# A message-passing layer: the first node tile alone and picked from SBUF, the split of h and the last bias through PSUM

## The chip, the core and the metric

The kernel runs on one core of a Trainium2 chip. A core has five engines with queues of their own, each executed in order: TensorE (PE, matmuls into PSUM), VectorE (DVE), ScalarE (ACT), GpSimd (POOL) and SyncE (SP), which issues most transfers. SBUF is the working memory, PSUM takes the matmuls' results, DRAM holds inputs, outputs and tables. The metric is the device time of one execution in microseconds (us), lower is better. Five runs of the kernel before gave 4235.94 to 4246.19, median 4244.6.

## The reference

12500 nodes with 128 features, 412500 edges sorted by their target node `dst`, 20 edge features, one weight an edge.

```python
h = maximum(layernorm(x), 0)
h = h @ W_in2f
Wij = (softplus(f_ij @ W_f1 + b_f1) - LOG2) @ W_f2 + b_f2
Wij = Wij * rcut_ij[:, None]
agg = segment_sum(h[dst] * Wij, src)          # called with idx_i = src, idx_j = dst
out = x + (softplus(agg @ W_o1 + b_o1) - LOG2) @ W_o2 + b_o2
```

`dst` is sorted, so the rows of h that a run of edges reads lie close together. `src` isn't, so the messages go to scattered places.

## The kernel before, in words

**Chunks.** The edges go in 806 chunks of 512, four to a group. Every chunk passes these stages, each a method of `Group`:

- `hidden` (L666): for two chunks at a time, `z = W_f1 @ f` on PE, K = 20, the two chunks in two groups of rows of the array; `hidden_log` (L675) three ScalarE activations of 1024 columns, `hidden_end` (L683) one VectorE product. The result is `r`.
- `bias` (L767) and `value` (L779): PSUM tile `v` = bias + r @ W_f2, four PE matmuls (8 instructions, since float32 goes in two passes). For the first chunks the bias is put in by PE (L772), later by ScalarE (L776).
- `rows` (L617): a window of 32 rows of h, each stored as three bfloat16 parts, is read from a table in DRAM into `near`, from a start that SP loads from memory; `window` (L760) compares the edges' node numbers (relative to the chunk's first, `rel`) with row numbers; `pick` (L787) is one matmul for each 128 edges, of the comparison with `near`; `picked` (L794) scales by `rcut` on ScalarE, four activations of 128 columns (L799).
- `blocks` (L690), `rank` (L698), `rank_end` (L715): where each message goes. `inb` marks the block of 128 target nodes, matmuls with triangular matrices (L711, and L744 for the chunk before) count the places taken, a reduction (L716) and three small operations give `slot`. `columns` (L629) makes the numbers for eight groups at once.
- `message` (L803): VectorE multiplies `v` and `hg` into `o` (L810), and GpSimd issues four indirect DMAs (L814), each putting 128 messages into `slots` in DRAM: 3224 in all.

**Collecting.** While chunks go on, `Collect` reads the filled segments of `slots` back and sums them by matmuls (L865, L886). The last segment is collected after the last chunk, followed by the output stage (`finish`, L427), which adds `x`. `x_ahead` (L1075) loads `x` early: from chunk 300 on, the first 14 sets get the last bias added by VectorE (L425, `x_bias`), the others by GpSimd after its last indirect DMA. Slots are cleared by transfers of 387 KB (L1185), spread over the steps: one each at steps 0, 1, 2, 4, 5, 7, 8, 9 and so on.

**h.** `make_h(q)` (L326) makes four node tiles of 128 rows in six stages, parted by `yield`: statistics on VectorE and 1/sqrt by Ln and Exp on ScalarE (L337 to L342); a refinement and the centring and scaling of x on VectorE (L346 to L353); transposes on PE and Relu on ScalarE (L358, L360); the product with W_in2f (L364) and the first bfloat16 part (L366); `left` = h minus that part, on VectorE (L369), and the second part (L370); the third part (L372: `left` minus the second, both in SBUF), and the stores to the tables. Table 0 holds the first 512 rows and serves chunks 0 to 8; table 1 (896 rows) needs the second set too and serves chunks from 9 on. `NEXT` (L914) is 8, the last chunk of table 0.

**Order.** The program's order is written out by hand: every engine executes its instructions in the order in which the code emits them. The prologue (L1154 to L1179) makes the first set and chunk 0's hidden part; then `step(k)` (L972) is called for k = -3, -2, ... Step k emits chunk k's `message`, k + 1's `picked` and `value`, k + 2's `pick` and `bias`, k + 3's `window`, and up to six chunks ahead of `rows`, `blocks` and `rank`. After step k one stage of the first two sets is emitted (from k = -1), from k = 6 on one stage of `side()` (L1141): later sets, further loads, `rest()`. PSUM's eight banks: z two, acc one, v three (bias, picks and values in turn), one for the counts, one for the constant `count_ps`. `o` has four buffers of two chunks, so VectorE can be up to eight chunks ahead of GpSimd.

Of the kernel before, what the change touches and what calls it, by code (L numbers as in the profile page):

```python
# [17 lines left out]
P = 128  # L18
TG = 16
CH = 512  # L20
# [13 lines left out]
FIRST = 64  # L34
NEAR = 2 * P
# [7 lines left out]
def gnn_kernel(  # L43
# [33 lines left out]
    NFLAG = 6 * len(SEGS) + 9  # L77
# [66 lines left out]
    nbo1 = sbuf("nbo1", [P, 1])  # L144
    before = sbuf("before", [P, P])
# [26 lines left out]
    rows_at = NPART * CH * 3 // 2 + CH  # L172

# [9 lines left out]
    def load_x(q):  # L183
        n = min(QT, NTILE - q * QT)
        full = min(n, N // P - q * QT)
        xb = ln.tile([P, QT, P], F32, name="xb")
        if full < n:
            nc.vector.memset(xb[:, full:n, :], 0.0)
            nc.sync.dma_start(xb[:N % P, full, :], x[q * QN + full * P:N, :])
        if full:  # L190
            nc.sync.dma_start(xb[:, :full, :], x[q * QN:q * QN + full * P, :]
                              .rearrange("(c p) f -> p c f", p=P))
        return xb

# [59 lines left out]
    def constants():  # L254

        early[0] = load_x(0)
        part_load(0)
        first_load(0)
        nc.sync.dma_start(win, w_in2f)

        for j in range(NCHUNK):
            nc.sync.dma_start(wf1[32 * j:32 * j + RBF, :], w_f1)

        nc.scalar.preload_act_table_set("natural_log_exp_and_others")
        nc.scalar.dma_start(bf1, b_f1[:, None])
        nc.scalar.dma_start(wf2, w_f2)
        nc.scalar.dma_start(bf2, b_f2[None, :].to_broadcast([P, P]))
        make_identity(nc, ident)
# [4 lines left out]
        nc.gpsimd.iota(prow_i, pattern=[[0, 1]], base=0, channel_multiplier=43)  # L273
        nc.gpsimd.iota(places, pattern=[[1, P]], base=0, channel_multiplier=0,
# [27 lines left out]
    def biases(psum):  # L302

        nc.vector.tensor_scalar(nbf1, bf1, -1.0, None, op0=ALU.mult)
        b12 = psum.tile([P, QT, P], F32, name="b12", tag="acc")[:, 0, :]
# [20 lines left out]
    def make_h(q, psum):  # L326

        n = min(QT, NTILE - q * QT)
        xb = early.pop(q, None)
# [6 lines left out]
        for i in range(n):  # L336
            nc.vector.bn_stats(st[:, i, :], xb[:, i, :])  # L337
            nc.vector.bn_aggr(mv[:, i, :], st[:, i, :])

        rs = ln.tile([P, QT], F32, name="rs")  # L340
        nc.scalar.activation(rs[:, :n], mv[:, :n, 1], AF.Ln, bias=eps)
        nc.scalar.activation(rs[:, :n], rs[:, :n], AF.Exp, scale=-0.5)  # L342
        yield

        ve = ln.tile([P, QT], F32, name="ve")
        nc.vector.tensor_scalar(ve[:, :n], mv[:, :n, 1], EPS, -0.5, op0=ALU.add, op1=ALU.mult)  # L346
        r2 = ln.tile([P, QT], F32, name="r2")
        nc.vector.tensor_mul(r2[:, :n], rs[:, :n], rs[:, :n])
        nc.vector.tensor_mul(r2[:, :n], r2[:, :n], ve[:, :n])
        nc.vector.scalar_tensor_tensor(rs[:, :n], r2[:, :n], 1.5, rs[:, :n],  # L350
                                       op0=ALU.add, op1=ALU.mult)
        for i in range(n):
            nc.vector.tensor_scalar(xb[:, i, :], xb[:, i, :], mv[:, i, 0:1], rs[:, i:i + 1],  # L353
                                    op0=ALU.subtract, op1=ALU.mult)
        yield
        xps = psum.tile([P, QT, P], F32, name="xps", tag="acc")
        for i in range(n):
            nc.tensor.transpose(xps[:, i, :], xb[:, i, :], ident)  # L358
        xT = ln.tile([P, QT, P], F32, name="xT")
        nc.scalar.activation(xT[:, :n, :], xps[:, :n, :], AF.Relu)  # L360
        yield
        hps = psum.tile([P, QT, P], F32, name="hps", tag="acc")
        for i in range(n):
            nc.tensor.matmul(hps[:, i, :], xT[:, i, :], win, start=True, stop=True)  # L364
        hb = ln.tile([P, QT, 3, P], BF16, name="hb")
        nc.scalar.activation(hb[:, :n, 0, :], hps[:, :n, :], AF.Copy)  # L366
        yield
        left = ln.tile([P, QT, P], F32, name="left")
        nc.vector.tensor_sub(left[:, :n, :], hps[:, :n, :], hb[:, :n, 0, :])  # L369
        nc.scalar.activation(hb[:, :n, 1, :], left[:, :n, :], AF.Copy)  # L370
        yield
        nc.vector.tensor_sub(hb[:, :n, 2, :], left[:, :n, :], hb[:, :n, 1, :])  # L372
        for (b, rows), table in zip(tables, h3_t):
            lo = max(0, b - q * QN) // P
            hi = min(n, (b + rows - q * QN) // P)
            if lo < hi:
# [4 lines left out]
                if b + rows == QN:  # L381
                    yield
# [5 lines left out]
            h3[q * QN:q * QN + n * P, :].rearrange("(c p) f -> p c f", p=P),  # L388
            hb[:, :n, :, :].rearrange("p c k f -> p c (k f)"))
# [32 lines left out]
    def x_bias(xo, pieces, engine=nc.vector):  # L422
        for p, cs, rows in pieces:
            xi = xo[:p, cs, :]
            engine.tensor_add(xi, xi, spread(bo2[:p, :], xi.shape[1]))  # L425

    def finish(t0, n, sT, quad, psum, z, xo=None, bank=("v", 3)):  # L427

        pieces = x_pieces(t0, n)
        if xo is None:  # L430
            xo = quad.tile([P, QT, P], F32, name="xo", bufs=6)
            x_load(xo, pieces)
            x_bias(xo, pieces)
# [103 lines left out]
    with tc.tile_pool(name="edge", bufs=2) as edge, tc.tile_pool(  # L537
# [11 lines left out]
        count_ps = state_ps.tile([P, P], F32, name="count_ps")  # L549
# [33 lines left out]
        class Group:  # L583


            def __init__(self, g):
# [3 lines left out]
                if g % NB == 0:  # L590
                    f = edge.tile([P, NB, CH], F32, name="f")
                    for j in range(NCHUNK):
                        nc.sync.dma_start(f[32 * j:32 * j + RBF, :, :],
                                          f_t[g:g + NB, j].rearrange("b k n -> k b n"))
                    kept["f"] = f
                self.f = kept["f"][:, g % NB, :]
                i = g - self.seg.g0
                if i % SB == 0:
# [3 lines left out]
                    nc.sync.dma_start(src_i[:, :w], src_t[:, cols])  # L602
                    rcut = edge.tile([P, SB * TG], F32, name="rcut")
                    nc.sync.dma_start(rcut[:, :w], rcut_t[:, cols])
# [3 lines left out]
                if g == 0:  # L608
                    rel_store(0)
                self.rel = edge.tile([WP, NCHUNK, CH], BF16, name="rel", bufs=4)  # L610
                nc.sync.dma_start(self.rel, rel_d[g * NCHUNK:(g + 1) * NCHUNK, :][None, :, :]
                                  .to_broadcast([WP, NCHUNK, CH]))
# [3 lines left out]

            def rows(self, c):  # L617

                k = self.g * NCHUNK + c
                t = table_of[k]  # L620
# [8 lines left out]
            def columns(self):  # L629
                if len(self.cols) == 3:  # L630
# [677 lines left out]
```

## Time and profile before

| what | value |
|---|---|
| profiled execution, whole | 4243.52 us |
| its span, first to last instruction | 4241.8 us |
| median of five runs | 4244.6 us |
| POOL busy | 3146.0 us, 74% of the span |
| PE busy | 3369.1 us, 79% |
| VectorE busy | 3093.4 us, 73% |
| ScalarE busy | 2774.7 us, 65% |
| HBM traffic | 192 GB/s over the span |

Busy times of PE overlap, since matmuls are pipelined. A group's row gives the line, engine and operation, out<-in by the program's names, the count, the busy time, the mean duration in ns, and the engine's idle time just before its instructions with what ended most of it. "issue" is idle time that ends without a wait that the profile shows. A timeline row merges equal neighbours: its duration is from the first's start to the last's end.

### The profile page before, as it was taken

Reading aid. Unit: us, or ns where it says so; the run is one execution under the profiler, and the core shown is the slowest. Engines: PE = TensorE matmul, PEld = TensorE weight load, DVE = VectorE, ACT = ScalarE, POOL = GpSimd, SP = SyncE. Lnnn points to the kernel's source line nnn. Section 1 sums busy time; section 2 is a strip of 40 time slices with the busy share of each in tenths; the row PEclk is TensorE's granted clock in tenths of the full one; section 3 lists DMA queues with packets and bytes.
Section 4 is the critical chain, followed back from the end, with each engine's and each line's share of the span. In section 5 each row is a group of like instructions: output and inputs, shape, how many; then the busy total and the mean of one; then the engine's idle time right before and its main releaser. Section 6 shows DMA issues by size and latency. Waiting matters only on the chain. (4 is left out here: it accounts for less than half of the span.)

```text
span 4241.8 us, 72525 instructions
## 1 busy us (share of the span) xinstructions
PE 3369.1 (79%) x21598; PEld 2617.0 (62%) x21598; DVE 3093.4 (73%) x6698; ACT 2774.7 (65%) x5464; POOL 3146.0 (74%) x3292
## 2 busy tenths in 40 slices
PE   6666676766776676678888888888888988988888
PEld 4444454444444444467777777777777777776777
DVE  7766665666555555567778777887888888888877
ACT  6776676677666666666666666666666666766644
POOL 5777777777777777777777777777777777777772
PEclk9777766776666666689899999998998998999999
DMA  6665555545444344467778766778776876787766
GB/s 185 193 185 182 171 165 181 162 149 176 131 127 119 106 147 149 145 185 230 218 216 258 235 206 211 218 215 264 222 213 205 266 243 189 234 245 202 207 203 178
DMA packets 515212, 820.54 MB, mean 193 GB/s; under 512 B 177188, under 2 KB 312728, under 8 KB 514812
## 3 DMA queue, kind: packets, MB, share of 16 engines
q1 hardware_dynamic: 411212, 602.55, 49.1%
q0 software_dynamic: 103168, 213.15, 15.0%
q8 instruction: 175, 2.87, 0.3%
q14 instruction: 225, 1.84, 0.1%
q10 hardware_dynamic: 432, 0.13, 0.0%
HBM read 419.75 MB, written 395.69 MB: 192 GB/s over the span
## 5 line engine op out<-in xcount | busy, mean ns | idle before, releaser
L814 POOL DMA_INDIRECT slots<-o,slot x3224 | 3108.5, 964 | 1011.6 <-issue 756.3
L886 PEld LDWEIGHTS acc<-to,m 128*128 128x128 f32 x8152 | 1077.3, 211 | 244.8 <-issue 148.6
L799 ACT ACTIVATE hg<-picked,rcut 128x128 f32<-128x128 f32 x3224 | 909.9, 364 | 391.0 <-PE picked L791 238.1
L783 PEld LDWEIGHTS v<-wf,r 128*128 128x128 f32 x6448 | 1010.0, 236 | 245.8 <-issue 154.0
L886 PE MATMUL acc<-to,m 128*128 128x128 f32 x8152 | 1138.7, 299 | 25.1 <-DVE to L865 21.6
L783 PE MATMUL v<-wf,r 128*128 128x128 f32 x6448 | 1086.3, 323 | 10.6 <-ACT v L776 10.6
L671 PE MATMUL z<-f,wf 20*128 20x512 f32 x1612 | 595.4, 822 | 409.3 <-DVE r L687 408.0
L776 ACT ACTIVATE v<-bf 128x512 f32<-128x512 f32 x804 | 483.8, 602 | 596.9 <-DVE o L810 577.8
L865 DVE TENSOR_TENSOR to<-count_ps,m 128x640 f32<-128x640 f32 (+3 forms) x793 | 632.2, 823 | 48.9 <-PE acc L886 42.8
L808 DVE COPY o<-place 128x8 f32<-128x8 f32 x403 | 80.7, 200 | 797.5 <-DMA slots<-o,slot 796.9
L791 PE MATMUL picked<-near,at 96*128 96x128 bf16 x3224 | 364.6, 244 | 368.5 <-DVE o L810 357.5
L810 DVE TENSOR_TENSOR o<-v,hg 128x512 f32<-128x512 f32 x806 | 549.2, 681 | 65.0 <-PE v L783 57.3
L791 PEld LDWEIGHTS <-at 96*128 96x128 bf16 x3224 | 292.3, 111 | 422.5 <-issue 397.3
L687 DVE SCALAR_TENSOR_TENSOR r<-z,nbf,a 128x1024 f32<-128x1024 f32 x403 | 512.9, 1273 | 45.1 <-ACT a L681 44.7
L678 ACT ACTIVATE a<-z,bf 128x1024 f32<-128x1024 f32 x403 | 443.8, 1101 | 139.3 <-PE z L671 139.3
L671 PEld LDWEIGHTS z<-f,wf 20*128 20x128 f32 x1612 | 148.2, 224 | 593.8 <-DVE r L687 564.5
L681 ACT ACTIVATE a<-a,half 128x1024 f32<-128x1024 f32 x403 | 462.8, 1148 | 13.1
L716 DVE TENSOR_REDUCE top<-free 128x4 f32<-128x392 f32 x806 | 445.2, 552 | 12.3 <-PE free L711 12.2
L692 DVE TENSOR_TENSOR inb<-count_ps,blk 128x392 f16<-128x392 f32 x806 | 443.7, 551 | 0.0
L679 ACT ACTIVATE a<-a 128x1024 f32<-128x1024 f32 x403 | 425.9, 1057 | 12.8
L744 PE MATMUL free<-inb,rest_of 128*128 128x392 f16 x806 | 309.1, 384 | 32.4 <-DVE top L716 21.6
L711 PE MATMUL free<-inb,after 128*128 128x392 f16 x806 | 310.1, 385 | 7.0 <-DVE inb L692 4.3
(115 smaller groups left out, 1359.4 us busy)
## 6 DMA issues: line engine op xcount, KB each, us to landing
m<-slots SPq DMA_DIRECT2D x307, 387.0 KB
m<-slots SPq DMA_DIRECT2D x278, 322.5 KB
rel<-rel_d SPq DMA_DIRECT2D x202, 384.0 KB
slots<-o,slot POOLq DMA_INDIRECT x3224
m<-slots SPq DMA_DIRECT2D x193, 258.0 KB
slots<-zero SPq DMA_DIRECT2D x96, 387.0 KB
f<-in_f_t SPq DMA_DIRECT2D x404, 80.0 KB
slots<-zero SPq DMA_DIRECT2D x58, 516.0 KB
```

The lines of the kernel that those rows point to most:

```text
L671: nc.tensor.matmul(z[:, k, :], wf1[rows, :], self.f[rows, :], start=True, stop=True)
L681: nc.scalar.activation(a, a, AF.Ln, bias=half, scale=0.5)
L687: nc.vector.scalar_tensor_tensor(r, z, nbf1, a, op0=ALU.max, op1=ALU.add)
L716: nc.vector.tensor_reduce(self.top[:, c * QT:(c + 1) * QT], free_v, axis=mybir.AxisListType.X, op=ALU.max)
L776: nc.scalar.activation(v, spread(bf12, QT), AF.Copy)
L783: nc.tensor.matmul(v[:, i, :], r[:, i * P:(i + 1) * P], wf2, start=False, stop=True, skip_group_check=True)
L791: nc.tensor.matmul(ps[:, i, :], at[:, i * P:(i + 1) * P], near, start=i == 0, stop=i == QT - 1, skip_group_check=True)
L799: nc.scalar.activation(hg[:, i, :], ps[:, i, :], AF.Copy, scale=self.rcut[:, j:j + 1])
L810: nc.vector.tensor_mul(o[:, :, :P], v, hg)
L814: put = nc.gpsimd.indirect_dma_start(out=views[j % VIEWS], out_offset=bass.IndirectOffsetOnAxis(ap=self.slot[:, j:j + 1], axis=0), in_=o[: ...
L865: nc.vector.tensor_tensor(to[:, :n, :], count_ps[:, None, :].to_broadcast([P, n, P]), m[:, :n, P:].to_broadcast([P, n, P]), op=ALU.is_equal)
L886: nc.tensor.matmul(self.acc[b // QT][:, i, :], m[:, j, :P], to[:, j, :], start=t == 0, stop=t == self.seg.tiles(b) - 1)
```

## The change

**First tile alone.** `make_h(0, psum, True)` makes node tile 0 by itself, from its own transfer `x_first`, and keeps its three parts in SBUF (`hb_first`). The other three tiles of the first set follow as `h0`. Chunks 0 to 5 (`DIRECT`) do not read a table: `window` compares their node numbers, spread over 128 partitions by DMA (`dst_near`), with the partition's number, and `pick` sums three matmuls for each 128 edges, one for each part. `near_check` later looks whether these chunks' numbers are all within 0 to 127, by two VectorE reductions over the 3072 numbers in one partition.

**Order.** Loads are issued anew: f, src, the weights and the broadcast numbers first, the rest of x behind. Chunks 0 to 3 pass z, logs and products one by one (`hidden_half`, `halves`) instead of in pairs; the prologue now ends with chunk 2's message, and steps begin at k = 2, with the clears of steps 0 to 2 issued there. Ranks and blocks run at first less far ahead; slots are made chunk by chunk for groups 0 to 2 (`LONE`), not for group 0 alone. The first set's last three tiles get four stages before step 2, two after step 3 and one after step 5; the second set's stages come once after steps 3 and 4 and twice after steps 5 and 6. Rows of chunk 9 on are issued from step 7 (before: from step 5).

**x centred by ScalarE, h split in PSUM, last bias from PSUM.** In `make_h` the mean is subtracted by ScalarE (`AF.Identity` with a bias) and the scale moves behind the product: the first part is a scaled copy, `left` is made in place in PSUM by one VectorE operation a tile, and the third part is subtracted with `left` read from PSUM. VectorE's `x_bias` reads the last bias from `bo2_ps` in PSUM, which shares a bank with `count_ps`; GpSimd's still reads SBUF.

```diff
@@ constants()
-        early[0] = load_x(0)
-        part_load(0)
-        first_load(0)
-        nc.sync.dma_start(win, w_in2f)
-        for j in range(NCHUNK):
-            nc.sync.dma_start(wf1[32 * j:32 * j + RBF, :], w_f1)
+        nc.sync.dma_start(x_first[:, 0, :], x[:P, :])
+        nc.scalar.dma_start(wf1[:RBF, :], w_f1)
...
+        group(0)
+        g = groups[0]
+        g.load_f(0)
+        g.load_f(1)
+        g.load_src()
+        nc.sync.dma_start(wf1[32:32 + RBF, :], w_f1)
+        near_load(0, 1)
+        g.load_rcut()
+        near_load(1, 3)
+        for j in (2, 3):
+            g.load_f(j)
+            nc.sync.dma_start(wf1[32 * j:32 * j + RBF, :], w_f1)
+        early[0] = load_x(0)
+        first_load(0)
+        part_load(0)
+        near_load(3, DIRECT)
@@ near_check()
+        row = dst_near[0:1, :, :].rearrange("p k e -> p (k e)")
+        over = early_row(5)[:, 1:2]
+        for i, op in enumerate((ALU.max, ALU.min)):
+            nc.vector.tensor_reduce(over, row, axis=mybir.AxisListType.X, op=op)
...
+            yield
@@ make_h
-        for i in range(n):
-            nc.vector.tensor_scalar(xb[:, i, :], xb[:, i, :], mv[:, i, 0:1], rs[:, i:i + 1],
-                                    op0=ALU.subtract, op1=ALU.mult)
+        nc.vector.tensor_scalar(nm[:, i0:n], mv[:, i0:n, 0], -1.0, None, op0=ALU.mult)
+        for i in range(i0, n):
+            nc.scalar.activation(xb[:, i, :], xb[:, i, :], AF.Identity, bias=nm[:, i:i + 1])
...
-        nc.scalar.activation(hb[:, :n, 0, :], hps[:, :n, :], AF.Copy)
+        for i in range(i0, n):
+            nc.scalar.activation(hb[:, i, 0, :], hps[:, i, :], AF.Copy, scale=rs[:, i:i + 1])
         yield
-        nc.vector.tensor_sub(left[:, :n, :], hps[:, :n, :], hb[:, :n, 0, :])
-        nc.scalar.activation(hb[:, :n, 1, :], left[:, :n, :], AF.Copy)
+        for i in range(i0, n):
+            nc.vector.scalar_tensor_tensor(hps[:, i, :], hps[:, i, :], rs[:, i:i + 1],
+                                           hb[:, i, 0, :], op0=ALU.mult, op1=ALU.subtract)
+        nc.scalar.activation(hb[:, i0:n, 1, :], hps[:, i0:n, :], AF.Copy)
         yield
-        nc.vector.tensor_sub(hb[:, :n, 2, :], left[:, :n, :], hb[:, :n, 1, :])
+        nc.vector.tensor_sub(hb[:, i0:n, 2, :], hps[:, i0:n, :], hb[:, i0:n, 1, :])
@@ window, pick
+                if k < DIRECT:
+                    nc.vector.tensor_scalar(at, dst_near[:, k, :], node, None, op0=ALU.is_equal)
...
+                if self.g * NCHUNK + c < DIRECT:
+                    parts = [hb_first[:, 0, j, :] for j in range(3)]
@@ step(k)
-            part("rows", min(k + LW, 2 * k + 3, NEXT if k < NEXT - 3 else NCH), rows)
+            part("rows", min(k + LW, NEXT if k < NEXT - 1 else NCH) if k > 3 else DIRECT - 1, rows)
...
-            upto = max(made["rank"], min(k + LR, 2 * k + 3))
+            upto = max(made["rank"], min(k + LR, k + 2 + max(0, k - 3) // 2))
@@ x_ahead, rest
-                    x_bias(*pending.pop(0), engine)
+                    x_bias(*pending.pop(0), b, engine)
...
+            nc.scalar.activation(bo2_ps, bo2, AF.Copy)
@@ the prologue and the steps
+            lone, h0, h1 = make_h(0, psum, True), make_h(0, psum), make_h(1, psum)
...
+            hgs[0] = g.picked(0, ps.pop(0))
...
+            g.message(0, vs.pop(0), hgs.pop(0))
...
+            g.message(1, vs.pop(1), hgs.pop(1))
...
+            g.message(2, vs.pop(2), hgs.pop(2))
+            for _ in range(4):
+                next(h0)
...
-            for k in range(-3, max(NCH, max(units) + 1)):
-                for seg, d in zeros.get(k, ()):
+            for k in range(2, max(NCH, max(units) + 1)):
+                for seg, d in sum((zeros.get(j, []) for j in range(0 if k == 2 else k, k + 1)), []):
...
-                if k >= -1:
-                    for m in h:
-                        next(m, None)
+                if k == 3:
+                    shift(0)
+                    next(h0)
+                    next(h0)
+                for _ in range((0, 0, 0, 1, 1, 2, 2)[k] if k < 7 else 1):
+                    next(h1, None)
+                if k == 5:
+                    next(h0, None)
```

## The prediction

> **What bounds the kernel now.** First the page's groups, for the engine that issues most; then GpSimd's (POOL's) timeline from its first transfer to its last; then what lies beside its longer transfers; last PE's and SP's timelines over the first 70 us. In a timeline line the columns are start, time, engine, line, operation, and in brackets the idle time before it with what ended that.
>
> ```profile
> L814 POOL DMA_INDIRECT slots<-o,slot x3224 | 3108.5, 964 | 1011.6 <-issue 756.3
> ```
> ```profile
> 26.24 1.18 POOL L814 DMA_INDIRECT slots<-o,slot  x1 [22.26 <-DVE o L810]
> ...
> 30.25 0.96 POOL L814 DMA_INDIRECT slots<-o,slot  x1 [0.31 <-issue]
> 37.94 0.96 POOL L814 DMA_INDIRECT slots<-o,slot  x1 [6.74 <-DVE o L810]
> 39.20 0.96 POOL L814 DMA_INDIRECT slots<-o,slot  x1 [0.30 <-issue]
> ...
> 126.73 0.96 POOL L814 DMA_INDIRECT slots<-o,slot  x1 [0.30 <-DMA slots<-o,slot]
> 127.99 1.68 POOL L814 DMA_INDIRECT slots<-o,slot  x1 [0.30 <-issue]
> ...
> 4123.06 0.96 POOL L814 DMA_INDIRECT slots<-o,slot  x1 [0.30 <-issue]
> ```
> Of the idle 1011.6 us, 22.26 and 6.74 precede the first and the fifth transfer; the other 982.6 are 0.30 or 0.31 each, between neighbours. So from 37.94 POOL never waits again: 0.957 + 0.305 = 1.262 us a transfer, 5.05 a chunk of four. Carried back over chunk 0, that stream "starts" at S = 37.94 - 5.05 = 32.9. The span is a sum:
>
> 32.9 + 3224 x 1.262 (4068.7) + 22.4 (transfers longer than 0.957) + 117.8 (after the last one, 4124.0 to 4241.8) = 4241.8.
>
> The execution took 4243.52, 1.7 outside the span; the median shown is 4244.6, so sums made here stand 1.1 below it. Only S, the 22.4 and the last stage can change the time. The last stage's code is as it was.
>
> **The lengthened transfers (h split in PSUM, last bias from PSUM).** I laid VectorE's timeline beside each longer transfer. The worst lie under one kind:
>
> ```profile
> 128.17 0.67 DVE L372 TENSOR_TENSOR hb<-left,hb 128x512 bf16<-128x512 f32 x1
> ```
> L372, a subtraction with both inputs in SBUF, runs 25 times; the 28 transfers beside it are 7.7 us longer in all (1.68 at 127.99 is one). L425, the bias added from SBUF, runs 14 times: 17 transfers, 4.1 us. L369, the same subtraction with one input in PSUM, takes 0.685 us as against 0.677 and costs the 32 transfers beside it 0.15. The change gives L372's successor and the 14 bias adds a PSUM input: 11.8 less some 0.4 is **11.4 us saved**. Bounds: 0 if a PSUM input doesn't free POOL (L372's rows), 11.8 if wholly. The edit's price, per set of four tiles: ScalarE gets four centrings of 0.28 (L1156's row) and four scaled copies of 0.28 for one of 0.59, +1.65; VectorE loses four L353 (1.12) and gains four 0.28 (L307's row) for L369's 0.68 and one 0.17, -0.5. None of these forms is in the trace: a centring or scaled copy lies between L1156's 0.28 and L799's 0.364, a 128x128 split with PSUM on both sides between L307's 0.28 and L353's 0.36; I take 0.28, since L799's four also finish in 1.14. With the upper ends a set costs ScalarE 0.7 and VectorE 0.3 more, under the same cover. After 100 us this hides under POOL (ScalarE is 0.65 to 0.75 busy, products lie 10 us and more ahead); before, it counts in the ramp.
>
> The Trainium skill, "SBUF — State Buffer", section "Who interferes with whom", says that GpSimd is held up by a VectorE instruction with two SBUF inputs, and also by tensor_scalar in a two-port mode. The first agrees with L372 and L425; by the second L353 should cost too, and moving it would save more, but the 36 transfers beside L353 are only 0.24 us longer in all, so the sum has nothing for it.
>
> **The ramp (first tile alone, six chunks from SBUF).** Durations are rows of the first 70 us. VectorE's constants end at 3.6 (L300). Statistics 0.5, Ln 0.30, Exp 0.21, centring 0.28: 4.8. Transpose 0.43, Relu 0.28, product 0.58: PE is free at 6.2. Then PE's order: one half of z 2.1 (L671's four take 2.08 because two row groups lie side by side; one alone saves nothing): 8.3; bias 2.07: 10.4; rank 0.5: 10.9; twelve picks 1.55 (L791's four take 0.64, each next 0.11): 12.4 (their comparison against int32 node numbers is L230's 0.49 for L763's 0.36, beside PE); value 2.08: 14.5; product 0.69 and hand-over 0.3: **first transfer at 15.5**, not 26.24. What waited for the table's way through DRAM is gone; late next is PE.
>
> Chunk 1: half 2.1, picks 1.55, pass and rank 0.9, value 2.08 on PE, with log and product of the half between: 22.5, and POOL has waited 1.9. Chunk 2, with two halves: 30. Then four stages for the first set's other three tiles stand in every queue ahead of chunk 3's value: VectorE 1.2 and 0.8, ScalarE 0.5, 0.85, 0.5, 0.85, PE 1.0 and 1.6, mostly one behind another: chunk 3 at 39. Chunk 4 needs a whole pair's logs (3.3), L687 (1.27) and a value behind that: 50. Before, it starts at 53.1, so 3 us are left of the 10.7.
>
> PE's speed is the first unknown:
> ```profile
> 37.59 2.08 PE L783 MATMUL v<-wf,r 128*128 128x128 f32 x8
> ...
> 48.25 1.06 PE L783 MATMUL v<-wf,r 128*128 128x128 f32 x8
> ```
> The same eight take 2.08 until 42.9 and 1.06 from there. I take half speed to 20 (PE is denser here). Between 20 and 43 about 7 us of the chain is PE at half speed and 3.5 at full, so half speed to 43 makes the ramp 3.5 longer; full speed from 14 saves half of the 3.4 between 14 and 20, 1.7.
>
> The Trainium skill, "TensorE: Matmul & The Clock Gate", Part 1, says that PE runs at half clock until about 3.4 us of sustained activity and falls back after an idle window. The two rows agree; by it the long wait below brings the clock down again, which speaks against this change and would add one or two us.
>
> Next the tables. Chunk 9 is the first that reads the table which the second set (h1) completes. Now h1's last stage runs at the end of step 6, and step 7 both issues near 9 and picks with it; before, two steps lay between. From before:
> ```profile
> 56.90 1.56 SPq L378 DMA_DIRECT2D h<-hb  x3
> ...
> 61.97 4.61 SPq L626 DMA_DIRECT2D near<-h  x4
> ```
> ```profile
> 66.39 0.40 PE L791 MATMUL picked<-near,at 96*128 96x128 bf16 x4 [1.12 <-DMA near<-h]
> ```
> VectorE's last split ended at 56.87 and near 9 came at 66.39: 9.5 us of SP issues (three tables, h3, two clears) and landings. Steps 4 to 6 at 5.1 us each, as in before (products at 41.3, 45.6, 51.1, 56.8), put that split at 65 and near 9 at 74.5. Behind the waiting pick stand, on PE, the ranks of 10 and 11; VectorE waits for these ahead of chunk 8's product: pick, pass and rank 1.0, top and slots 1.15, product 0.85, 0.3: **chunk 8 at 77.7**, S = 77.7 - 40.4 = 37.3.
>
> Last near_check: two reductions over 3072 elements in one partition. Rows for 512 and 744 elements take 0.67 and 0.92, so 3.4 each, on VectorE in steps 11 and 12. The lead then is about 4.4 us (3.9 a chunk against 5.05, as in before from 65.4 to 80.8), so some 2.7 show: **S = 40**. Clears 0 to 2, now issued together at step 2, SP's later group loads, and per-chunk slots for groups 1 and 2 (0.6 each) lie within these steps.
>
> Sum: 40 + 4068.7 + (22.4 - 11.4) + 117.8 + 1.7 = **4239**, 4.3 below the profiled execution: 11.4 saved, 7.1 given back.
>
> Bounds of S: low 28.5 (PE at full speed from chunk 1, near 9 after 4.35 us as near 0 at 20.54 after 16.19, the check hidden): 4228. High 47 (half speed to 43, the check bare): 4246.
>
> **Rivals.** 0.2% (8.5 us, 4235 to 4252) is about what a measurement of this kernel can tell from no change.
> - Forecast: 4239, itself 4233 to 4246. Chance 0.52.
> - The ramp's gain holds: PE soon fast, near 9 quick; S 28.5. For it: SP's queue is emptier than at 56.90. Against: pick and issue share a step. 4228, faster. Chance 0.31.
> - The change doesn't do what it says: PSUM inputs still hold POOL up; L425's 4.1 alone is saved. Against: L369's row. 4243.5 + 7.1 - 4.1 = 4246. Chance 0.11.
> - Slower: the wait at pick 9 leaves PE at half speed over steps 7 to 14. There PE needs 2.1 value, 0.6 pick, 0.9 ranks, 1.05 z: 4.7 of 5.05, so no lead grows, and all one-time VectorE work is paid by POOL: the check 6.8, the second shift (L214 to L219 on 744 elements, 4.7), slow steps 3.5. S = 37.3 + 15 + 2 = 54: 4253. It decides against the change from S = 44.3 on. For it: ramp rows at 2.08; against: 1.06 from 48 on. Chance 0.06.
>
> Faster by over 0.2%: the second case and 0.05 of the first, 0.36. Slower: 0.06. Between: 0.58. The range leaves out the last case and the ends: 4226 to 4247.
>
> **What would show it.** POOL's first transfer near 15.5; waits before chunks 1 to 4 and chunk 8; the pick of chunk 9 ended by a near load; two VectorE reductions of 3.4 us near 95 to 105; later no POOL wait, and no transfer above 1.2 us beside the splits and the bias adds. Wrong if POOL has no wait after chunk 4, or if transfers under the new split stay long.

## The result, and the profile after

The changed kernel takes 4249.0 us (median of 24 runs, 4240.4 to 4255.2) against 4240.4 for the kernel before (44 runs): a ratio of 1.0020, 95% interval 1.0014 to 1.0025, some 8.5 us slower. The forecast was 4239 in a range up to 4247. The profiled execution took 4248.24 us, its span 4246.5, against 4243.52 and 4241.8 before: here the two lie 4.7 apart, since the profiled execution of before was 3.1 above its median.

Runs a1 to b4 below fell in an hour in which every kernel, that of before too, took about 5300 us, and TensorE, VectorE and ScalarE stood still together for some 500 us in all (pieces of over 1 us), where these kernels otherwise have about 70; of the kernels with the new ramp, in which the added stops begin after 75 us, only what lies before that is used, no time of these eight runs is (their ratios to before in that hour are 1.0015 to 1.0080, the port edits alone 1.0037 and 1.0028), and all questions but a4's were put again.

First the page's group of GpSimd's transfers, then GpSimd's timeline: seven of the eleven transfers ahead of which it waited over 0.4 us (chunks 0, 4, 6, 7, 8, 12 and 13), the others left out.

```profile
L905 POOL DMA_INDIRECT slots<-o,slot x3224 | 3095.7, 960 | 1033.6 <-issue 750.3
```
```profile
15.69 1.18 POOL L905 DMA_INDIRECT slots<-o,slot  x1 [11.63 <-DVE o L901]
...
54.63 0.95 POOL L905 DMA_INDIRECT slots<-o,slot  x1 [6.05 <-DVE o L901]
69.61 0.96 POOL L905 DMA_INDIRECT slots<-o,slot  x1 [5.18 <-DVE o L901]
77.53 0.95 POOL L905 DMA_INDIRECT slots<-o,slot  x1 [3.17 <-DVE o L901]
89.57 0.96 POOL L905 DMA_INDIRECT slots<-o,slot  x1 [7.30 <-DVE o L901]
...
114.40 0.95 POOL L905 DMA_INDIRECT slots<-o,slot  x1 [3.26 <-DVE o L901]
120.85 0.96 POOL L905 DMA_INDIRECT slots<-o,slot  x1 [1.72 <-DVE o L901]
```

The group's line is nearly that of before: 4 ns less a transfer and 22.0 us more idle time. The timeline says where. The first transfer is 10.5 us earlier, and then the stream stops ahead of chunks 2, 3, 4, 6, 7, 8, 10, 12 and 13; before, it never stopped after chunk 1. Call a chunk's **lateness** the start of its first transfer less 5.05 us for each chunk ahead of it: 15.7 at chunk 0, 34.4 at chunk 4, 42.2 at 7, 49.2 at 8, 55.2 at 13 and from there on only what longer transfers add. Before it is 26.2 at chunk 0 and 32.9 from chunk 1 on. So the ramp's 10.5 us of head start is gone at chunk 4, and 22.0 are lost at chunk 13, where before stands at 33.2.

The sum: by the two lines of the group GpSimd idles 22.0 us more (1033.6 for 1011.6) and its transfers take 12.8 less (3095.7 for 3108.5). Behind the last transfer come 113.2 us for 117.8, 4.6 less. Together that is 4.6 of the 4.7 us by which the spans differ.

TensorE's timeline at chunks 6 and 9:

```profile
61.11 0.61 PE L880 MATMUL picked<-near,at 96*128 96x128 bf16 x4 [8.51 <-DMA near<-h]
...
62.30 2.08 PE L727 MATMUL z<-f,wf 20*128 20x512 f32 x4
64.31 2.08 PE L868 MATMUL v<-wf,r 128*128 128x128 f32 x8
...
85.87 0.61 PE L880 MATMUL picked<-near,at 96*128 96x128 bf16 x4 [8.28 <-DMA near<-h]
```

Two picks, not one, wait for rows of a table, 8.51 and 8.28 us. Behind the first one stand the ranks, the next z and the value of chunk 6: nothing of these needs the table, but TensorE takes its instructions in order. What pick 6 waits for is in VectorE's and the DMA queue's timelines (SPq is SyncE's queue):

```profile
51.56 0.56 DVE L414 TENSOR_TENSOR hb<-hps,hb 128x384 bf16<-128x384 f32 x1 [1.94 <-ACT hb L412]
```
```profile
52.14 0.40 SPq L420 DMA_DIRECT2D h<-hb  x1
...
56.71 2.60 SPq L679 DMA_DIRECT2D near<-h  x3
```

The first set's last split ends at 52.1, its table is issued at 52.14, a clear and the next loads of f and rel behind it (SP issues these until 55.6), the rows of chunk 6 at 56.71, and the pick starts at 61.11: 9.0 us from split to pick. From the second set's split (75.97 to 76.66) to pick 9 it is 9.2.

The new split now lies beside transfers of the usual length; VectorE's and GpSimd's timelines at one of its 26 places:

```profile
128.92 0.68 DVE L414 TENSOR_TENSOR hb<-hps,hb 128x512 bf16<-128x512 f32 x1
```
```profile
128.43 0.96 POOL L905 DMA_INDIRECT slots<-o,slot  x1 [0.30 <-issue]
129.69 0.95 POOL L905 DMA_INDIRECT slots<-o,slot  x1 [0.30 <-issue]
```

Over all 28 such transfers the excess is 0.16 us (7.7 before), beside the 14 bias adds (L468) 0.0 (4.1 before).

### The profile page after: what moved, and what is told of

Its sections match the earlier page's. It is cut to its first block, busy times and chain, and to the rows that moved or that the text cites. A ratio compares the mean times of both kernels' runs of the same rounds, so it can differ in the third digit from the quotient of the medians.

```text
span 4246.5 us, 72807 instructions
## 1 busy us (share of the span) xinstructions
PE 3371.2 (79%) x21644; PEld 2619.5 (62%) x21644; DVE 3102.7 (73%) x6728; ACT 2819.8 (66%) x5647; POOL 3133.3 (74%) x3293
## 5 line engine op out<-in xcount | busy, mean ns | idle before, releaser
L905 POOL DMA_INDIRECT slots<-o,slot x3224 | 3095.7, 960 | 1033.6 <-issue 750.3
L868 PE MATMUL v<-wf,r 128*128 128x128 f32 x6448 | 1089.7, 324 | 21.6 <-ACT v L861 18.1
L956 DVE TENSOR_TENSOR to<-numbers,m 128x640 f32<-128x640 f32 (+3 forms) x793 | 632.1, 823 | 48.4 <-PE acc L977 40.4
L880 PEld LDWEIGHTS <-at 96*128 96x128 bf16 (+1 forms) x3272 | 297.6, 112 | 404.0 <-issue 365.1
L746 ACT ACTIVATE a<-z,bf 128x1024 f32<-128x1024 f32 (+1 forms) x405 | 444.6, 1098 | 137.2 <-PE z L727 128.1
L748 ACT ACTIVATE a<-a,half 128x1024 f32<-128x1024 f32 (+1 forms) x405 | 463.4, 1144 | 13.2
L772 DVE TENSOR_TENSOR inb<-numbers,blk 128x392 f16<-128x392 f32 x806 | 443.6, 551 | 0.0
L747 ACT ACTIVATE a<-a 128x1024 f32<-128x1024 f32 (+1 forms) x405 | 426.3, 1053 | 12.9
L824 PE MATMUL free<-inb,rest_of 128*128 128x392 f16 x806 | 310.1, 385 | 32.4 <-DVE top L796 20.9
```

The source lines that it names most:

```text
L748: nc.scalar.activation(a, a, AF.Ln, bias=half, scale=0.5)
L868: nc.tensor.matmul(v[:, i, :], r[:, i * P:(i + 1) * P], wf2, start=False, stop=True, skip_group_check=True)
L880: nc.tensor.matmul(ps[:, i, :], at[:, i * P:(i + 1) * P], rows, start=i == 0 and j == 0, stop=i == QT - 1 and j == len(parts) - 1, skip_gr ...
L905: put = nc.gpsimd.indirect_dma_start(out=views[j % VIEWS], out_offset=bass.IndirectOffsetOnAxis(ap=self.slot[:, j:j + 1], axis=0), in_=o[: ...
L956: nc.vector.tensor_tensor(to[:, :n, :], count_ps[:, None, :].to_broadcast([P, n, P]), m[:, :n, P:].to_broadcast([P, n, P]), op=ALU.is_equal)
```

## The experiments

The theory after the result: the edits of the operands are worth about what they were priced at; the ramp lost more than forecast because picks 6 **and** 9 wait for tables in TensorE's in-order queue, because the check is paid almost bare, and to a smaller part because TensorE runs at half clock. Rivals: TensorE's half clock makes every step of the ramp slow, whatever the picks wait for; the operand edits slow the ramp by ScalarE's extra operations; the shorter transfers have nothing to do with the operands.

"Lengthened" is the time of all 3224 transfers above 0.957 us each. The expectations' figures for it (23.75 before, 13.6 saved) are another count of the same thing; by this one it is 23.1 and 12.8.

| kernel | lateness at chunk 4 | 7 | 8 | 13 | lengthened, us | last stage, us | ratio to before (95%) |
|---|---|---|---|---|---|---|---|
| before | 32.9 | 32.9 | 32.9 | 33.2 | 23.1 | 117.8 | 1 |
| changed kernel | 34.4 | 42.2 | 49.2 | 55.2 | 10.3 | 113.2 | 1.0020 (1.0014, 1.0025) |
| d1: port edits, ramp of before | 33.8 | 34.2 | 34.3 | 34.3 | 11.8 | 112.7 | 0.9975 (0.9964, 0.9986) |
| d3: new ramp, old operands | 36.1 | 43.2 | 51.7 | 55.0 | 20.9 | 120.3 | 1.0046 (1.0032, 1.0059) |
| c1: no wait of pick 6 | 36.0 | 38.7 | 45.2 | 48.2 | 10.8 | 113.5 | 1.0012 (1.0003, 1.0022) |
| e1: no wait of pick 9 | 34.2 | 41.6 | 42.9 | 48.4 | 10.1 | 114.5 | 1.0009 (1.0000, 1.0019) |
| d4: no check | 31.4 | 38.8 | 45.8 | 47.6 | 9.2 | 114.0 | 1.0010 (1.0001, 1.0019) |
| c2: neither wait, no check | 33.1 | 33.4 | 33.4 | 33.4 | 10.2 | 110.7 | 0.9985 (0.9975, 0.9995) |
| e2: values in bfloat16 | 33.5 | 39.4 | 46.1 | 49.2 | 9.5 | 113.9 | 1.0009 (1.0000, 1.0019) |
| d2: no waits, check later | 34.3 | 34.6 | 36.0 | 37.0 | 10.2 | 115.8 | 0.9977 (0.9968, 0.9987) |

All columns but the last come from one profiled execution of each kernel, the ratio from the medians of all its executions. Five of the ten profiled ones lie within 1 us of their kernel's median; those of before and d3 lie 3.1 and 4.7 us above it, those of d1, d4 and c2 3.6, 2.6 and 8.6 below. So a sum of the columns gives a larger or smaller difference than the ratio does.

### The port edits alone (a1, b1, d1)

The kernel before, with the new `make_h` forms and the bias from PSUM:

```diff
-        for i in range(n):
-            nc.vector.tensor_scalar(xb[:, i, :], xb[:, i, :], mv[:, i, 0:1], rs[:, i:i + 1], ...)
+        for i in range(n):
+            nc.scalar.activation(xb[:, i, :], xb[:, i, :], AF.Identity, bias=nm[:, i:i + 1])
...
-        nc.vector.tensor_sub(left[:, :n, :], hps[:, :n, :], hb[:, :n, 0, :])
+        for i in range(n):
+            nc.vector.scalar_tensor_tensor(hps[:, i, :], hps[:, i, :], rs[:, i:i + 1],
+                                           hb[:, i, 0, :], op0=ALU.mult, op1=ALU.subtract)
...
-            x_early = x_ahead(early_homes(), nc.vector)
+            x_early = x_ahead(early_homes(), bo2_ps, nc.vector)
```

> The kernel before, with its own ramp, and all the port edits (x centred by ScalarE, h split in PSUM, last bias from PSUM). Theory: the 13.6 us that the lengthened transfers lost between the two traces belong to these edits alone, and the ramp of the change gave 22 back: this kernel is 13 us faster than before (4227 where before is 4240), up to 18 if the 4.6 us shorter last stage is theirs too; transfers over 1.15 us fall from 24 to about 4. Rival: the transfers got shorter because the later stream stood otherwise against VectorE's work, not by the operands: then the lengthened transfers stay near 23 us and the time at 4240.

> The kernel before, with its own ramp, and all the port edits: the same text as in the run of the ports alone, on another chip. Where POOL's stream sets the time (no waits of POOL after chunk 1), theory: 13 us faster than before, up to 18 if the shorter last stage belongs to these edits; lengthened transfers 10 to 12 us in all instead of 23.75, about 4 over 1.15 us instead of 24. Rival (not the operands, but how the stream stood against VectorE's work): no difference, lengthened transfers near 23 us.

> The kernel before, with its own ramp, and all the port edits. Theory: the 13.6 us of shorter transfers belong to these edits alone and the ramp stays: 13 us faster than before, up to 18 if the 4.6 us shorter last stage is theirs too; lengthened transfers 10 to 11 us in all instead of 23.75, lateness after chunk 5 at 33 as before. Rival (the edits' eight short ScalarE operations a set slow the ramp): lateness 35 or more, 8 to 11 us faster.

GpSimd's timeline of d1, the first and the last wait after the first transfer:

```profile
38.33 0.96 POOL L818 DMA_INDIRECT slots<-o,slot  x1 [6.00 <-DVE o L814]
...
59.44 0.96 POOL L818 DMA_INDIRECT slots<-o,slot  x1 [0.70 <-DVE o L814]
```

The old ramp stays but for 1.3 us (three waits of 0.44 to 0.70 that were not there), the lengthened transfers fall by 11.3 us, the last stage is 5.1 shorter, and by the ratio the kernel is 0.25% (some 10 us) faster than before. The edits are good by themselves.

### The new ramp alone (a2, d3)

The reverse: the changed kernel with the forms of before in `make_h` and `bo2` in the early adds.

> The changed kernel with its new ramp, but x centred by VectorE, h split through SBUF and the last bias from SBUF as before. Theory: the ramp alone costs 22 us less what the last stage gives: 18 to 22 us slower than before (4258 to 4262), lateness of POOL's stream about 55 after chunk 13, lengthened transfers near 23 us. Rival (the port edits themselves slow the ramp, by ScalarE's eight short operations a set): lateness near 45, some 8 to 12 us slower than before.

> The changed kernel with its new ramp, but x centred by VectorE, h split through SBUF and the last bias from SBUF as before: the ramp alone. Theory: lateness after chunk 13 stays at 54 to 56 and the lengthened transfers are back at 22 to 25 us: 12 to 14 us slower than the changed kernel, 18 to 22 us slower than before. Rival (the port edits slow the ramp): lateness 45 to 50, within 8 us of the changed kernel.

VectorE and GpSimd in d3 where the old subtraction is back (L411, both inputs in SBUF):

```profile
161.82 0.67 DVE L411 TENSOR_TENSOR hb<-left,hb 128x512 bf16<-128x512 f32 x1
```
```profile
161.64 1.69 POOL L902 DMA_INDIRECT slots<-o,slot  x1 [0.31 <-DVE at L845]
```

One transfer takes 1.69 instead of 0.96, as beside L372 before. In all, the transfers beside L411 are 5.2 us longer and those beside the 14 old bias adds 5.0. The lateness at chunk 13 is that of the changed kernel (55.0 and 55.2): the operand edits do not slow this ramp. 0.46% slower than before is the ramp's price alone, 19.5 us.

### Without the check (a3, b2, d4)

```diff
-            yield from near_check()
+            yield
+            yield
```

> The changed kernel without the check of the first six chunks' node numbers (two reductions over 3072 elements on VectorE; the flag that they would set is left at zero). Theory: POOL's waits before chunks 12 and 13 (3.26 and 1.72 us) go: 5.0 us faster than the changed kernel. Rival (PE at half clock sets the steps there, the reductions lie beside it): 0 to 2 us.

> The changed kernel without the check of the first six chunks' node numbers (two reductions over 3072 elements on VectorE; the flag that they would set is left at zero). Theory: POOL's waits of 3.26 and 1.72 us before chunks 12 and 13 go, lateness after chunk 13 is 50 to 51 instead of 55.2: 4 to 5 us faster than the changed kernel. Rival (TensorE at half clock sets those steps and the reductions lie beside it): 0 to 2 us.

> The changed kernel without the check of the first six chunks' node numbers (the flag that it would set is left at zero). Theory: POOL's waits of 3.26 and 1.72 us before chunks 12 and 13 go, lateness after chunk 13 is 50 to 51 instead of 55.2: 4 to 5 us faster than the changed kernel, at the time of before or a little under. Rival (slow steps set POOL there and the reductions lie beside them): 0 to 2 us.

VectorE's timeline of the changed kernel, at the check and the products around it:

```profile
109.62 3.33 DVE L212 TENSOR_REDUCE early_room<-early_room 1x1 f32<-1x3072 int32 x1
...
113.44 0.68 DVE L901 TENSOR_TENSOR o<-v,hg 128x512 f32<-128x512 f32 x1
...
116.44 3.33 DVE L212 TENSOR_REDUCE early_room<-early_room 1x1 f32<-1x3072 int32 x1
```

The product of chunk 12 (at 113.44) comes straight behind the first reduction and its transfer 1.0 later; chunk 13's likewise behind the second. From chunk 10 to 13 the changed kernel's lateness grows by 4.4 (50.8 to 55.2), d4's by 0.1: the check costs 4.3 us. The times say the same within their intervals (0.10%, 4.2 us). The other 3.4 by which d4 is earlier at chunk 8 are not the check's: 2.1 of them are there from chunk 2 on, 3.0 at chunk 4, and they come under the clock below.

### Pick 6, pick 9, both (c1, b3 and e1, c2)

c1 picks chunks 6 and 7 from SBUF too (their numbers reach 126 here):

```diff
-DIRECT = 6
+DIRECT = 8
...
+        near_load(6, 8)
```

e1, and b3 before it, let the first table serve as far as chunk 24, and spread the second set's stages:

```diff
-        table_of.append(0 if n < QN - NEAR - P else min(n // QN, NQ - 1) + 1)
+        table_of.append(0 if n < QN - P else min(n // QN, NQ - 1) + 1)
...
-                for _ in range((0, 0, 0, 1, 1, 2, 2)[k] if k < 7 else 1):
+                for _ in range(int(k > 3)):
```

c2 does both, without the check.

> The changed kernel with eight chunks picked from SBUF instead of six (the destinations of chunks 6 and 7 lie in another piece of SBUF, and the check covers the first six only, as before). The first table is then needed by chunk 8 and not by chunk 6. Theory of the tables (each of the two picks that wait for a table stops TensorE's whole queue for some 8.4 us, and POOL pays it in full): the wait of 8.51 us ahead of pick 6 goes, lateness at chunk 6 is 34 to 36 instead of 39.3, at chunk 7 34 to 37 instead of 42.2, and the wait ahead of pick 9 stays near 8 us. Theory of the clock and of slow steps: lateness at chunk 7 stays at 40 or more.

> The changed kernel with the first table of h used up to chunk 24 instead of chunk 8, and the stages of the second set of tiles one to a step from step 4 on, so that no pick of the ramp waits for that set. Theory of the table: the 8.28 us wait of pick 9, and with it the 7.30 us wait of POOL before chunk 8, goes; lateness at chunk 8 is 42 to 44 instead of 49.2, after chunk 13 48 to 50 instead of 55.2: 5 to 7 us faster than the changed kernel. Theory of the clock (TensorE at half clock makes each step 7 to 8 us, whatever the pick waits for): lateness after chunk 13 stays at 52 or more, 0 to 3 us faster.

> The changed kernel with the first table used up to chunk 24 and the second set's stages one to a step: pick 9 has no wait for a table left, pick 6 keeps its own. Theory of the tables: lateness at chunk 7 as in the changed kernel (41 to 43), at chunk 8 42 to 43 instead of 49.2, after the check 45 to 48 instead of 55.2; 7 to 9 us faster than the changed kernel. Theory of the clock: lateness at chunk 8 is 46 or more, 0 to 4 us faster.

> Eight chunks picked from SBUF, the first table used up to chunk 24, the second set's stages one to a step, and no check of the direct chunks' node numbers (the flag that it would set is left at zero): no pick of the ramp waits for a table. Theory of the tables: lateness at chunk 8 is 35 to 38 instead of 49.2, and from there the lead grows; what is left against the kernel before (32.9) is the ramp up to chunk 4 (34.4). Theory of the clock and of slow steps: lateness at chunk 8 is 43 or more.

GpSimd's and TensorE's timelines of c1 around chunks 6 to 9, then of e1:

```profile
67.64 0.96 POOL L907 DMA_INDIRECT slots<-o,slot  x1 [1.67 <-DVE o L903]
74.03 0.96 POOL L907 DMA_INDIRECT slots<-o,slot  x1 [1.64 <-DVE o L903]
85.55 0.95 POOL L907 DMA_INDIRECT slots<-o,slot  x1 [6.78 <-DVE o L903]
```
```profile
69.66 0.39 PE L882 MATMUL picked<-near,at 96*128 96x128 bf16 x4
81.85 0.61 PE L882 MATMUL picked<-near,at 96*128 96x128 bf16 x4 [8.86 <-DMA near<-h]
```
```profile
71.89 0.95 POOL L905 DMA_INDIRECT slots<-o,slot  x1 [7.58 <-DVE o L901]
83.28 0.96 POOL L905 DMA_INDIRECT slots<-o,slot  x1 [1.59 <-DVE o L901]
```
```profile
62.79 0.61 PE L880 MATMUL picked<-near,at 96*128 96x128 bf16 x4 [8.73 <-DMA near<-h]
```

Each kernel loses the one wait and keeps the other. In c1 GpSimd's waits ahead of chunks 6 and 7 shrink from 5.18 and 3.17 to 1.67 and 1.64; in e1 the one ahead of chunk 8 from 7.30 to 1.59. The lateness at chunk 13 falls by 7.0 and by 6.8. c1's lateness at chunk 7, 38.7, is above the 34 to 37 expected, with the ramp already 1.6 later at chunk 4 than in the changed kernel. From chunk 4 to 7 it loses 2.7, the changed kernel 7.8: 5.1 of these are the wait's. By the times c1 is 0.08% and e1 0.11% faster than the changed kernel, some 3 and 5 us, with intervals of 4 us either way; for e1 7 to 9 were expected.

GpSimd's timeline of c2, all its waits over 0.4 us after the first transfer but that ahead of chunk 3:

```profile
33.50 0.96 POOL L907 DMA_INDIRECT slots<-o,slot  x1 [7.08 <-DVE st L378]
...
53.30 0.96 POOL L907 DMA_INDIRECT slots<-o,slot  x1 [4.64 <-DVE o L903]
58.61 0.96 POOL L907 DMA_INDIRECT slots<-o,slot  x1 [0.57 <-DVE o L903]
```

After chunk 5 nothing stops the stream: lateness is 33.4 instead of 55.2 at chunk 13, 21.8 less. This was the fastest of c2's ten executions; by the ratios c2 is 0.35% (some 15 us) faster than the changed kernel. The three parts one by one (7.0, 6.8, 4.3) make 18.1. Of the 3.7 left, 1.3 is there at chunk 4 (33.1 for 34.4); the others belong to none of the parts alone. Probably products get ahead once the waits are gone, and cover what a step costs now and then; TensorE's clock is higher then too (below).

### TensorE's clock (a4, b4, e2)

a4 keeps TensorE busy with products that nobody reads; b4 and e2 take work from it (`wf2_b` is W_f2 in bfloat16, `n` is 14):

```diff
+                    fill(8)
                 vs[k + 1] = g.value(c, bs.pop(k + 1))
...
+                nc.tensor.matmul(numbers[:, 2 * P:3 * P], ident, ident, start=True, stop=True, ...)
```
```diff
-                    nc.tensor.matmul(v[:, i, :], r[:, i * P:(i + 1) * P], wf2,
+                    nc.tensor.matmul(v[:, i, :], r[:, i * P:(i + 1) * P],
+                                     wf2_b if self.g * NCHUNK + c < n else wf2,
```

> The changed kernel with extra products of the identity with itself on TensorE (into unused columns of a PSUM bank, nobody reads them) ahead of each value and each pick up to step 11: 8 at a time, 30 ahead of the picks of chunks 6 and 9. Theory (TensorE's half clock from 17 to 108 us is what made the ramp 15 us longer than predicted): the granted clock stays near 1.00 from 20 us on, the lateness after chunk 13 falls from 55.2 to 42 to 47, and the time by 8 to 13 us. Rival (the way through the tables sets the ramp: h0 and h1, their transfers, and VectorE's one-time work): the clock rises but the waits before chunks 6 and 8 stay, lateness 52 to 56, time within 3 us of the changed kernel or above it by what the products take.

> The changed kernel with the value products of the first 14 chunks in bfloat16 (the softplus of these chunks and W_f2 rounded to bfloat16, so these chunks' messages are less exact): four products that take some 0.5 us at half clock instead of 2.08 in float32. It takes about 1.5 us a chunk from TensorE without touching any wait or its clock. Theory of the clock (TensorE at half clock sets the ramp): lateness at chunk 8 falls from 49.2 to 40 to 43, after chunk 13 from 55.2 to 44 to 48: 7 to 11 us faster than the changed kernel. Theory of the table and of VectorE's one-time work: 0 to 3 us faster.

> The changed kernel with the value products of the first 14 chunks in bfloat16 (the softplus of these chunks and W_f2 rounded, so these chunks' messages are less exact): some 1.5 us a chunk less for TensorE, every wait as it was. Theory of the tables with a small share for the clock: lateness at chunk 4 is 31 to 33 instead of 34.4, after chunk 13 50 to 53 instead of 55.2, the waits ahead of picks 6 and 9 stay at 8 to 9 us; 2 to 5 us faster than the changed kernel. Theory of the clock: lateness after chunk 13 is 44 to 48, 7 to 11 us faster.

a4 was badly sized: eight such products take 1.95 us at full clock, not at half, so each batch cost about what it gave. Chunk 2 came at 31.60 (33.25 in the changed kernel), chunk 3 at 44.35 (43.85), and pick 6 still waited 2.50 us behind 6.86 us of filling; its granted clock did rise (0.90 from 25 to 50 us, 0.57 in the changed kernel), but it settles nothing on the clock's price. e2 lies between the two theories: 6.0 us less lateness at chunk 13 for some 1.5 us less TensorE work in each of 14 chunks, 0.9 of it at chunk 4, 3.1 at chunk 8, with the two picks waiting 10.11 and 8.95. So with both waits left, TensorE's own work at half clock still counts.

What speaks against the clock as the main cause is c2. Two stretches of 25 us, in the changed kernel and then in c2; the columns behind the stretch are its length, busy us (with instructions) of PE, PEld, DVE, ACT and POOL, the granted clock, the DMA share and GB/s:

```profile
25.00:50.00 25.00, 17.57 (x77) 11.72 (x77) 13.74 (x45) 17.44 (x37) 8.53 (x9) 0.57 0.36 122
50.00:75.00 25.00, 15.14 (x72) 10.90 (x69) 14.70 (x48) 12.98 (x31) 11.49 (x12) 0.57 0.45 138
```
```profile
25.00:50.00 25.00, 17.36 (x75) 11.32 (x75) 13.89 (x45) 17.22 (x36) 8.82 (x10) 0.57 0.33 108
50.00:75.00 25.00, 18.39 (x115) 13.74 (x114) 20.22 (x65) 17.76 (x40) 16.28 (x17) 0.77 0.76 229
```

Up to 50 us the clock is the same 0.57, the values of chunks 0 to 4 take about 2.0 us in both, and c2 loses nothing behind chunk 5. From there the two part: 0.57 and 0.77 up to 75 us, 0.57 and 0.79 from 75 to 100. So taking the waits away also raises the clock, and c2 doesn't tell what a wait costs by itself from what the half clock behind it costs. There is a price of the clock without any wait, too. d4 had, by chance, a stretch at full clock where the changed kernel had half, at the halves of z for chunks 2 and 3; TensorE's row for the first of these in the changed kernel, then in d4 (the second took 2.07 and 1.12):

```profile
19.98 2.07 PE L736 MATMUL z<-f,wf 20*128 20x512 f32 x2
```
```profile
20.27 1.29 PE L736 MATMUL z<-f,wf 20*128 20x512 f32 x2
```

Chunk 2 came 2.06 us earlier in d4 (31.19), chunk 4 at lateness 31.4 instead of 34.4.

### A whole kernel without the waits (d2)

c2 with the check of all eight chunks back (four reductions), but started at step 18 instead of 11; the loads and one-time operations that follow it in `rest()` move with it:

```diff
-                if i >= 5 and next(others, 1) and not quads and 2 + i // 9 >= NQ:
+                if i >= 12 and next(others, 1) and not quads and 2 + i // 9 >= NQ:
```

> A whole kernel that computes everything: the change with eight chunks from SBUF, the first table used up to chunk 24, the second set's stages one to a step, and the check of all eight chunks' node numbers seven steps later, when the products lie ahead of POOL. Theory: no wait of POOL after chunk 5, lateness 33 to 34 after chunk 13, as in the run without any check: 6 to 8 us faster than before (4231 to 4233 where before is 4239). Rival (the lead is still smaller than a reduction of 3.3 us): 2 to 5 us of waits near chunks 19 to 22.

0.9977 (0.9968 to 0.9987): 0.23% faster than before and about 0.4% faster than the changed kernel. GpSimd still waits 1.72 ahead of chunk 8 and 1.25 ahead of chunk 10, but nowhere at the check: lateness stays 37.0 to 37.1 from chunk 10 to chunk 23. The 33 to 34 that were expected are missed by these two waits and by the ramp up to chunk 5 (34.6). d1 and d2 both beat both kernels and are not to be told apart. The ramp of before with the new operands is the simpler of the two: all the new order reaches, once it is mended, is the old lateness of 33 to 37.

## Why the prediction was wrong

**Port saving: right.** 11.4 us were forecast, 12.8 measured in the pair, 11.3 in d1, and 10.6 come back in d3, where the edits are undone. L372's and L425's excess of 11.8, with 0.16 and 0.0 us left beside their successors, makes up most of it. The Trainium skill's second rule ("SBUF — State Buffer", section "Who interferes with whom"), by which VectorE's centring could have cost too, was rightly given no term: in d3, where the centring is VectorE's again, 10.2 of the 10.6 us lie beside the other two forms.

**First transfer: right.** 15.5 forecast, 15.69 measured.

**Ramp up to chunk 4: mis-sized by 4.6 us** (lateness 34.4 for 29.8). The step was "I take half speed to 20". The changed kernel had full speed from some 14 to 17 us (the twelve picks at 15.84 take 0.84, at 21.98 again 1.46) and near 42, but none of the values of chunks 0 to 4 fell there. TensorE's timeline at the values of chunks 4 and 5:

```profile
47.65 2.08 PE L868 MATMUL v<-wf,r 128*128 128x128 f32 x8
...
51.45 1.15 PE L868 MATMUL v<-wf,r 128*128 128x128 f32 x8
```

The bound that the text gave for half speed to 43 was 3.5; the z and the value at 45.64 and 47.65 (2.07 and 2.08, in before 1.13 and 1.06 at 46.20 and 48.25) add 2.0. These 5.5 are more than the 4.6, so the clock can account for it, but no run shows that it is all of it. The Trainium skill's rule ("TensorE: Matmul & The Clock Gate", Part 1), that the clock falls back after an idle window, agrees with what follows the wait of pick 6 (z 2.08 at 62.30), and the two halves of z in d4 (1.29 and 1.12 for 2.07 each, chunk 2 earlier by 2.06) show what it costs here. The other half of the rule, full clock after some 3.4 us of activity, which the prediction took to agree with its two rows, doesn't come out: in before TensorE ran from 20.54 to 30.04 without a gap at half speed (the values at 23.06 and 28.13 take 2.08 and 1.91), and in the changed kernel it was busy 12.54 of the 15 us from 60 to 75, all at a granted clock of 0.50.

**The failing step: "What waited for the table's way through DRAM is gone", and behind it "Steps 4 to 6 at 5.1 us each, as in before".** The wait had not gone but moved, from chunk 0 to chunk 6, the first chunk that reads a table: the table has to be complete, and it is made by the first set's other three tiles, whose stages stand behind chunk 2. From that set's last split to pick 6 it took 9.0 us, close to the 9.5 that the prediction had worked out for the second set. From chunk 4 to 7 lateness grew by 7.8 us, for which the sum had nothing. c1 takes this one wait away and is 7.0 us less late at chunk 13. The text looked for the wait where the second set's stages were moved and did not ask the same of the first set.

**Pick 9: right.** 9.5 us forecast from split to pick, 9.2 measured; 7.5 us of lateness forecast (29.8 to 37.3), 7.0 measured from chunk 7 to 8, 6.8 taken away in e1. Only it all happened 12 us later, since the slower ramp and pick 6 lay ahead of it (split at 76.7 for 65).

**Check: mechanism right, cover wrong.** Two reductions of 3.33 (3.4 forecast), of which 4.3 were paid and not 2.7: there was no lead of 4.4 us by then. Slow steps cost a further 1.7 at chunk 10.

**Slower rival: nearly the result, by chance.** Its S of 54 and its time of 4253 stand beside 55.2 and 4248. It laid the loss on TensorE's half speed over steps 7 to 14, behind pick 9, and the clock was low there (0.57 from 75 to 100 us). But it put 15 us there, where lateness grew by 6.0 (49.2 to 55.2), 4.3 of it by the check; and it had no wait at pick 6. c1, e1 and d4 each take back a part of the loss, and c2 all of it; how much of a wait's part is the half clock behind it stays open.

**Last stage: left at 117.8, measured 113.2.** The eight undisturbed profiles with the new operands have 110.7 to 115.8, the two with the old ones 117.8 and 120.3. So it goes with these edits; by what way, no run here shows.

The terms together: 4.6 in the ramp up to chunk 4, 7.8 at pick 6, -0.5 at pick 9 and 3.3 at the check and the steps beside it make the 15.2 by which S was too low (55.2 for 40). Against it stand 0.7 of lengthened transfers (10.3 for the 11.0 of the sum) and 4.6 of the last stage: 9.9, where the forecast's sum (4239.2) and the profiled execution (4248.24) are 9.0 apart; the 0.9 left is under 0.0003 us a transfer, the rounding of 1.262 and 0.957.

## What to carry to other kernels

When an early start is bought by reading the first data from nearby, look for the first consumer that still takes the long way: the wait moves to it, and it costs as much there unless products have got ahead by then. In an engine that takes its instructions in order, one waiting pick stops everything behind it, so ask of each moved producer how many steps lie between its last stage and its first reader. And try the parts of a change alone: here an edit worth 0.25% was hidden under a reordering that cost 0.46%.

## What the runs showed of the hardware

- A VectorE subtraction with an input in PSUM leaves GpSimd's transfers alone (28 transfers, 0.16 us in all), with both inputs in SBUF one transfer takes up to 1.69 instead of 0.96; four 128x128 forms that read and write PSUM in place (L410) take 1.52 to 1.54 us, 0.34 to 0.36 each, and cost the transfers beside them 0.04 us in all.
- Rows that were written to DRAM and read back were in use 9.0 and 9.2 us after the last value was made, whichever set it was: in the first case 4.6 us passed from the table's issue to that of the rows and 4.4 from there to the pick.
- The changed kernel and d4, whose code is the same up to there, had half or full clock in the same 4 us of the ramp (z 2.07 and 1.12), which moved the third chunk by 2 us.
